# A four-layer convolution kernel: the start of its attention layer rearranged (factors spread by TensorE, input in eight pieces, small loads on another queue, first step's multiply on VectorE)

## The chip, the cores and the metric

The kernel runs on one core of one Trainium2 chip. The metric is the device time of one execution in microseconds; three runs of the kernel before gave a median of 10,728.44 us (10,727.74 to 10,730.07). The engines are named as the profile names them: PE (matrix products; PEld is its weight load), DVE (VectorE), ACT (ScalarE), POOL (GpSimd) and SP (SyncE, which issues DMA loads and stores). SPq and ACTq are the queues on which SP and ACT issue DMAs; q1 in the profile is SP's, q10 is ACT's.

## The reference

A tensor x of 8 images, 16 channels, 128 by 128 pixels, float32, goes through four layers, each of the form x + layer(groupnorm(x)), with 8 groups of two channels. The first layer, which the change concerns, makes of each pixel three tokens (one for each column of its 3x3 window, wrapped at the edges), each of 48 values (16 channels times three rows), and runs a small transformer block over them:

```python
x = _fold_to_kernels(in_x)               # (B*H*W, 3, 48)
qkv = _ln(x) @ w_attn.T                  # 4 heads of 12
att = softmax(einsum('nhtd,nhsd->nhts', q, k) / sqrt(12))
x = x + (att @ v) @ w_attn_proj.T
x = x + gelu(_ln(x) @ w_fc.T) @ w_fc_proj.T
x = sum(_ln(x), axis=1)
out = einsum('bhwc,oc->bohw', x, conv_w) + conv_b
```

The second layer is a gated 1x1 convolution (five 16x16 weights, five biases), the third a convolution of rational functions, the fourth one of splines. The change leaves the mathematics of all four as it is.

## The kernel before

**Constants and small loads.** The constants lie in one array; `const` holds those of the later layers and `const0` those of layer 0 (`center` to `last`). ACT's queue first issues `const` (L133), then small loads: the helper `rep` (L168 to L173) copies a bias of 16 values into each 16 of 128 partitions, one DMA each, for the two biases `bias0` and `bias3` and the five `b1s`; L224 puts each 16x16 weight of the second layer eight times on the diagonal of a 128x128 tile, the first two of them transposed. Together these are 96 DMAs. None of them is read in layer 0 except `bias0`, when a step's result is stored.

**Statistics.** The input arrives as eight pieces `xj` of 128 partitions by 2,048 values (1 MB each), loaded by SP (L240) into a pool of two buffers; VectorE takes four `bn_stats` of each (L242). `group_stats` (L178) aggregates them, sums over channel pairs with two small matmuls, takes the root on ACT (`lut`, L152) and gives a factor `rs0` and a shift `d0` for each of the 128 image-channel rows.

**Factors.** Layer 0 works on pairs of images: 128 partitions are two images with three rows of a window and 16 channels each, in two halves of 64, and which image lies in which half alternates with the number of the pair. The factors therefore have to move to other partitions. They are written to memory (`aff_d`, L267) and read back by 24 DMAs of SP (L275) into `aff`. For each of four pairs k, VectorE places the shifts in `shift` (L317), PE forms `pb` (L321), and VectorE makes `wcen`, the centering weights with the normalization folded in (L322). Behind the factors on the queues, weights are loaded (`wqkv`, `wfc`, `wcv`, `wpc`, `wfp`, `wfq`); `centered` (L290) subtracts a mean from the last three.

**Steps and rounds.** A step is four image rows of all images; 32 steps pass through a software pipeline in rounds n = -2 ... 34. In one round step n+2 (`ahead`) is loaded and centered, step n+1 (`then`) gets its queries, keys and values, its products with `multiply` and its scores, step n (`new`) its attention (`attend`), projection and half of its hidden layer, step n-1 (`old`) the rest, and step n-2 (`done`) is stored. So round 0 is the first with a `new` and has no `old`, and round -1 has a `then` and no `new`. `load` (L411) fills `xin`, one buffer of four pairs, by six DMAs for each pair (more at the image's edge); `center` (L425) reads it, so the rows of the next step wait for the centering of the one before. `multiply` (L464) forms the products of queries with shifted keys on POOL into tiles of a pool named "large" of five buffers, which `scores` (L479) sums on PE. `attend` (L511) spreads one row of the attention by three matmuls into banks 1 to 3, VectorE multiplies them with the values (L518), and POOL adds the three products of one pair (L527). `project` (L529) reads the sum; `two` (L336) hands out pairs of the eight PSUM banks, from bank 4 on while a `new` step attends.

**Order.** PE's instructions of layer 0 are tied in the order of the text by `in_turn`; VectorE's and POOL's long ones too, each on its own chain. All other instructions are put in order when the program is built: on each engine and queue, what is written earlier goes first among what is ready.

Of the kernel before, what the change touches and what calls it, by code (L numbers as in the profile page):

```python
# [36 lines left out]
def _constants():  # L37
# [23 lines left out]
    for k in range(4):  # L61
        for u in range(3):
            v = 32 * (2 * (k % 2) + u % 2) + 8 + 4 * (u // 2) + 2 * (k // 2)
            last[v + g, u, 32 * k + 16 * g + c] = 1.0
    parts["spread"] = spread.reshape(128, 512)
    parts["bcast"] = bcast.reshape(128, 640)
    parts["last"] = last.reshape(128, 384)
    p = np.arange(BC)
    parts["pair"] = 0.5 * (p[:, None] // 2 == p[None, :] // 2)
# [31 lines left out]
def kernel(  # L101
# [64 lines left out]
    nc.gpsimd.memset(eps_t, EPS)  # L166

    def rep(vec, n, name):  # L168

        t = cpool.tile([n * C, 1], F32, name=name)  # L170
        for b in range(n):
            nc.scalar.dma_start(t[b * C : (b + 1) * C], vec.unsqueeze(1))
        return t  # L173
# [45 lines left out]
    for n in range(5):  # L219
        t = cpool.tile([BC, BC], F32, name=f"w1_{n}")  # L220
        nc.gpsimd.memset(t, 0.0)
        for b in range(B):
            r = slice(b * C, (b + 1) * C)
            nc.scalar.dma_start(t[r, r], w1[n].rearrange("i o -> o i") if n < 2 else w1[n])  # L224
        w1s.append(t)
        b1s.append(rep(b1[n], B, f"b1_{n}"))
# [7 lines left out]
    with ExitStack() as l0:  # L234
        wp = l0.enter_context(tc.tile_pool(name="w0", bufs=1))
        with tc.tile_pool(name="x0", bufs=2) as xp:
            bn0 = xp.tile([BC, NCH, 6], F32, name="bn0", bufs=1)
            for j in range(8):
                t = xp.tile([BC, HW // 8], F32, name="xj")
                nc.sync.dma_start(t, xv[:, bass.ts(j, HW // 8)])  # L240
                for i in range(NCH // 8):
                    nc.vector.bn_stats(bn0[:, NCH // 8 * j + i], t[:, bass.ts(i, 512)])  # L242
            mean0, _, rs0, d0 = group_stats(bn0, "0")
        lo, hi = _WHERE["center"][1], _WHERE["last"][2]
        const0 = wp.tile([128, hi - lo], F32, name="const0")
        nc.scalar.dma_start(const0, const_in[:, lo:hi])

# [14 lines left out]

        aff_d = dram.tile([BC, 2], F32, name="aff_d")
        aff_s = wp.tile([BC, 2], F32, name="aff_s")
        nc.vector.tensor_copy(aff_s[:, 0:1], rs0)
        nc.vector.tensor_copy(aff_s[:, 1:2], d0)
        nc.sync.dma_start(aff_d, aff_s)  # L267
        aff = zeros([2, NP], "aff")
        for a in range(2):
            src = aff_d[:, a : a + 1].rearrange("(d p g c) a -> p g c (d a)", p=2, g=2, c=C)  # L270
            for odd in range(2):
                for g in range(2):
                    for i in range(3):
                        r = 64 * (g ^ odd) + 16 * i
                        nc.sync.dma_start(aff[r : r + 16, a, odd::2], src[odd, g])  # L275

# [4 lines left out]
        for i in range(3):  # L281
            for g in range(2):
                r = slice(64 * g + i * 16, 64 * g + i * 16 + 16)
                nc.scalar.dma_start(
                    wqkv[r, :, :E], w0_qkv[i].rearrange("c (n o) -> c n o", n=3)
                )
                nc.sync.dma_start(wfc[r], w0_fc[i])
                nc.scalar.dma_start(wcv[r, g * 16 : (g + 1) * 16], w0_conv[i])

        def centered(t):  # L290

            s = wp.tile([128, 1], F32, name="csum", bufs=3)
            nc.vector.tensor_reduce(s, t[:, :E], AX.X, ALU.add)
            nc.vector.tensor_scalar_mul(s, s, -1.0 / E)
            nc.vector.tensor_scalar(t[:, :E], t[:, :E], s, None, ALU.add)
# [3 lines left out]
        for g in range(2):  # L299
            nc.sync.dma_start(wpc[64 * g : 64 * g + E, :E], w0_proj)  # L300
            nc.scalar.dma_start(wfq[64 * g : 64 * g + 64, :E], w0_fcp[128:192])
# [23 lines left out]

        xin = wp.tile([128, NP, 512], F32, name="xin")
        nc.gpsimd.memset(xin, 1.0)
        act = l0.enter_context(tc.tile_pool(name="act0", bufs=1))
# [74 lines left out]
        class Step:  # L403
# [7 lines left out]
            def load(self, d):  # L411
                for k in (2 * d, 2 * d + 1):
                    for g in range(2):
                        for i in range(3):
                            r, lo = 64 * (g ^ (k % 2)) + i * 16, self.h0 + i - 1
                            a = max(-lo, 0)
                            z = min(H - lo, 4)
                            src, dst = x_in[2 * k + g], rows(xin[r : r + 16, k])
                            nc.sync.dma_start(dst[:, a:z], src[:, lo + a : lo + z])
                            if a:  # L420
                                nc.sync.dma_start(dst[:, 0:a], src[:, H - a : H])
                            if z < 4:
                                nc.sync.dma_start(dst[:, z:4], src[:, 0 : 4 - z])

# [38 lines left out]

            def multiply(self, d):  # L464

                for k in range(2):
                    parts = []
                    for at, n in ((0, 3), (3, 2)):
                        t = large("pd")
                        ins = nc.gpsimd.tensor_mul(  # L470
                            t[:, :n].rearrange("p n (a b) -> p n a b", a=4),
                            rows(self.q[d][:, k]).unsqueeze(1).to_broadcast([128, n, 4, W]),
                            windows(self.k[d][:, 4 * k : 4 * k + 4], at, n),
                        ).ins
                        in_turn("pool", ins)
                        parts += [t[:, i] for i in range(n)]
                    self.pd[2 * d + k] = parts
# [32 lines left out]

            def attend(self, k, j):  # L511

                for u in range(3):
                    r = slice(32 * u, 32 * u + 32)
                    pe(banks[:, 1 + u], spread[r, k], self.att[r, j], start=True, stop=True)
                y = large("y")
                v = self.v[k // 2][:, 4 * (k % 2) : 4 * (k % 2) + 4]
                ins = nc.vector.tensor_mul(  # L518
                    y.rearrange("p n (a b) -> p n a b", a=4),
                    banks[:, 1:4].rearrange("p n (a b) -> p n a b", a=4),  # L520
                    windows(v, j, 3),
# [134 lines left out]
        for n in range(-2, NCH + 3):  # L656
# [40 lines left out]
            if ahead:  # L697
                for d in range(2):
                    ahead.load(d)
            ring["from"] = 2 if new else 1  # L700
            for i, fs in enumerate(between):
                if new:
                    new.attend(i // 3, i % 3)
                for f in fs:
# [6 lines left out]
            if then:  # L711
                then.multiply(0)
                then.qkv(1)
                then.multiply(1)
            if ahead:
# [769 lines left out]
```

## Time and profile before

| | |
|---|---|
| Median of three runs | 10,728.44 us |
| The profiled execution, whole | 10,728.63 us |
| Its span in the profile | 10,726.8 us |
| Mean granted clock of TensorE | 0.976 |
| Busy over the span: PE, DVE, ACT, POOL | 84%, 81%, 80%, 52% |
| First bn_stats begins, last one ends | 6.59 us, 46.3 us |
| Root on ACT begins | 63.00 us |
| First centering on PE begins | 86.05 us |
| First multiply on POOL begins, last of that step ends | 104.42 us, 126.7 us |
| First attend on PE begins, first projection begins | 144.67 us, 174.68 us |
| Step 0's result added to the input (L588) | 369.3 us |
| Last step's result added to the input | 3,417.6 us |

The span is what the profiler saw between the first and the last instruction; the execution's own time lies 1.8 us above it. The last two rows bound the steady part of layer 0: 31 rounds. The rest of the span, some 7,300 us, belongs to the other three layers. A line of the timeline gives start, duration, engine, line of the source, operation and tiles, how many were put together, and in brackets how long the engine had been idle before it and what ended that.

### The profile page before, as it was taken

The page shows a single profiled execution, that of the slowest core. Times are in us where ns is not written, and L with a number is a line of the kernel's source. Part 1 is how long each engine was busy: PE and PEld are TensorE (multiplying, and loading weights), DVE is VectorE, ACT ScalarE, POOL GpSimd, SP SyncE. Part 2 cuts the span into 40 slices and gives each one's busy share as a digit, 9 for nine tenths or more (in the row PEclk, how much of TensorE's full clock was granted, in tenths as well). Part 3 has the DMA queues.
Part 4 walks back from the last instruction along what each step waited for, and adds up shares of the span by engine and source line. Part 5 has one row for each costly group of instructions (what it writes and reads, how often), then busy time and mean ns, then how long its engine had stood idle before and what let it go on. Part 6 is the DMA issues. An engine that isn't in the chain of part 4 may idle for free.

```text
span 10726.8 us, 191623 instructions
## 1 busy us (share of the span) xinstructions
PE 9016.0 (84%) x81588; PEld 2440.6 (23%) x81588; DVE 8720.1 (81%) x6829; ACT 8613.6 (80%) x7107; POOL 5545.4 (52%) x2681
## 2 busy tenths in 40 slices
PE   4999999999998568888888888888888888888799
PEld 1222222222222112222222222222222222222222
DVE  3555555555555569999999999999999999999977
ACT  2555555555554679999999999999999999999988
POOL 3655655555553555555555555555555555555522
PEclk8999999999999789999999999999999999999999
DMA  1000000000001320000000000000000000000022
GB/s 50 14 14 12 16 13 14 15 13 13 16 10 44 96 87 8 14 7 8 14 8 7 14 8 8 14 7 8 14 8 8 14 8 7 14 8 8 7 62 61
DMA packets 189456, 205.04 MB, mean 19 GB/s; under 512 B 46776, under 2 KB 155448, under 8 KB 186552
## 3 DMA queue, kind: packets, MB, share of 16 engines
q1 hardware_dynamic: 179944, 190.68, 6.7%
q8 instruction: 641, 10.50, 0.4%
q10 hardware_dynamic: 8656, 2.11, 0.1%
q14 instruction: 215, 1.76, 0.1%
HBM read 107.15 MB, written 60.04 MB: 16 GB/s over the span
## 4 chain that ended last, share of the span: by engine, by line
DVE 42%; PE 24%; issue 21%; ACT 7%; POOL 3%; DMA 2%; SPq 1%; ACTq 0%; DVEq 0%; POOLq 0%
PE banks L360 18%; DVE u L1030 15%; DVE pn L1030 10%; DVE u L1034 8%; DVE y L518 2%; DVE t L1020 2%; PE pn L971 2%; PE pd L971 2%; PE acc L1334 1%; POOL y L527 1%; DVE x L538 1%; ACT u L152 1%; DMA yd<-y 1%; ACT hid L152 1%; SPq L1298 1%
## 5 line engine op out<-in xcount | busy, mean ns | idle before, releaser
L1043 POOL TENSOR_TENSOR v<-t,u 128x1280 f32<-128x1280 f32 x1152 | 3374.3, 2929 | 2990.1 <-DVE t L1020 2960.8
L971 PE MATMUL pd<-f,wb 32*64 32x512 f32 x18432 | 2518.4, 610 | 332.8 <-ACT t L1009 301.0
L1020 DVE SCALAR_TENSOR_TENSOR t<-t,u 128x2048 f32<-128x2048 f32 x1152 | 2637.5, 2289 | 34.8 <-ACT u L152 25.2
L1009 ACT ACTIVATE t<-pd 128x1024 f32<-128x1024 f32 x2304 | 2348.6, 1019 | 86.6 <-POOL v L1043 42.3
L152 ACT ACTIVATE u<-u 128x2048 f32<-128x2048 f32 x1152 | 2200.4, 1910 | 0.0
L152 ACT ACTIVATE u<-t 128x2048 f32<-128x2048 f32 x1152 | 2192.1, 1903 | 0.0
L971 PE MATMUL pn<-f,wa 32*64 32x512 f32 x18432 | 1324.8, 624 | 938.4 <-DVE u L1034 938.1
L1030 DVE TENSOR_TENSOR u<-pn,u 128x1280 f32<-128x1280 f32 x1152 | 1718.1, 1491 | 39.4
L152 ACT ACTIVATE hid<-banks 128x1024 f32<-128x1024 f32 x576 | 571.4, 1023 | 1046.6 <-PE banks L360 1044.7
L527 POOL TENSOR_TENSOR y<-y 128x1536 f32<-128x1536 f32 x256 | 894.7, 3495 | 830.9 <-DVE y L518 830.9
L1062 PE MATMUL acc<-u,const 128*32 128x512 f32 (+2 forms) x13824 | 1118.9, 456 | 0.0
L1030 DVE TENSOR_TENSOR pn<-pn,u 128x768 f32<-128x768 f32 x1152 | 1104.2, 959 | 0.0
L1034 DVE SCALAR_TENSOR_TENSOR u<-t,pn 128x768 f32<-128x768 f32 x1152 | 1087.6, 944 | 0.0
L518 DVE TENSOR_TENSOR y<-banks,vp 128x1536 f32<-128x1536 f32 x384 | 672.9, 1752 | 274.0 <-PE banks L360 271.8
L971 PEld LDWEIGHTS pd<-f,wb 32*64 32x64 f32 x18432 | 512.1, 131 | 1610.2 <-ACT t L1009 1548.7
L1062 PE MATMUL acc<-v,const 128*32 128x512 f32 (+1 forms) x9216 | 749.9, 443 | 1.5 <-POOL v L1043 1.5
L544 ACT ACTIVATE sq<-x 128x1024 f32<-128x1024 f32 x384 | 397.9, 1054 | 412.3 <-DVE x L538 289.7
L971 PEld LDWEIGHTS pn<-f,wa 32*64 32x64 f32 x18432 | 279.5, 131 | 1947.3 <-DVE u L1034 1936.7
L470 POOL TENSOR_TENSOR pd<-q,kp 128x1536 f32<-128x1536 f32 (+1 forms) x256 | 693.6, 2733 | 8.0 <-PE banks L360 7.2
L360 PE MATMUL banks<-att,const 32*128 32x512 f32 x2304 | 497.3, 667 | 173.5 <-DVE att L509 95.9
L360 PE MATMUL banks<-h,wfc 64*128 64x512 f32 (+1 forms) x3072 | 618.4, 631 | 14.5 <-DVE h L606 14.5
L606 DVE TENSOR_TENSOR h<-banks,x 128x1024 f32<-128x1024 f32 x192 | 232.6, 1211 | 435.5 <-ACT hid L152 230.4
(182 smaller groups left out, 8068.9 us busy)
## 6 DMA issues: line engine op xcount, KB each, us to landing
f<-yd SPq DMA_DIRECT2D x512, 101.6 KB
yd<-y SPq DMA_DIRECT2D x320, 130.0 KB
xin<-in_x SPq DMA_DIRECT2D x752, 32.0 KB
four<-sil SPq DMA_DIRECT2D x256, 65.0 KB
xj<-in_x SPq DMA_DIRECT2D x8, 1024.0 KB
xl<-in_x SPq DMA_DIRECT2D x32, 256.0 KB
x1d<-xl SPq DMA_DIRECT2D x32, 256.0 KB
x<-x1d SPq DMA_DIRECT2D x8, 1024.0 KB
```

The source lines that it names most:

```text
L152: ins = nc.scalar.activation(out_, in_, func, **kw).ins
L360: in_turn("pe", mm(*args, skip_group_check=True, **kw).ins)
L470: ins = nc.gpsimd.tensor_mul(t[:, :n].rearrange("p n (a b) -> p n a b", a=4), rows(self.q[d][:, k]).unsqueeze(1).to_broadcast([128, n, 4, W]),
L518: ins = nc.vector.tensor_mul(y.rearrange("p n (a b) -> p n a b", a=4), banks[:, 1:4].rearrange("p n (a b) -> p n a b", a=4), windows(v, j, 3),
L527: in_turn("pool", nc.gpsimd.tensor_add(self.y[k], self.y[k], y).ins)
L971: yield mm(p[64 * (u % 2) : 64 * (u % 2) + 64, u // 2], w[lo : lo + 32, q % 2, n].rearrange("p c f -> p (c f)"), fs[g * NP + q][lo : lo + ...
L1009: in_turn("act", nc.scalar.activation(self.t[:, ab], self.pd, AF.Abs).ins)
L1020: ins = nc.vector.scalar_tensor_tensor(self.t, self.t, 1.0, self.u, op0=ALU.add, op1=ALU.mult).ins
L1030: in_turn("dve", nc.vector.tensor_mul(u if cols.start else p, p, u).ins)
L1034: ins = nc.vector.scalar_tensor_tensor(u, t, 2.0, p, op0=ALU.subtract, op1=ALU.mult).ins
L1043: ins = nc.gpsimd.tensor_mul(self.v, t, u).ins
L1062: ins = mm(accs[k][32 * q : 32 * q + 32, lo % 512 : (hi - 1) % 512 + 1], gather[:, int(part == 1), g], flat(c.u)[:, ab, lo:hi] if src is N ...
```

## The change

It has seven parts.

1. The factors no longer go through memory. Two new constants, `pairs` (which pair of images a row belongs to) and `pick` (which partitions it goes to), let VectorE make two scaled copies and PE spread them with two matmuls; one copy brings the result to `aff`.
2. The pool of input pieces has eight buffers instead of two.
3. `const0` is loaded and `xin` allocated and set to one before the pieces instead of behind the statistics and the weights.
4. The 96 small loads are collected in a list and issued by SP in round 0, behind the loads of step 2 in the text. `wfc` and `wpc` are loaded by ACT instead of SP.
5. `centered` is ordered behind the copy to `aff`.
6. Step 0's rows are loaded by SP for even pairs and by ACT for odd ones.
7. The `multiply` of the first step (round -1, with no `new`) is done by VectorE instead of POOL; the first seven `attend` calls of round 0 alternate between banks 1 to 3 and 4 to 6.

```diff
+    pick = np.zeros((128, 2, 128))
+    for odd in range(2):
+        for i in range(3):
+            pick[p, odd, 64 * (p // C % 2 ^ odd) + 16 * i + p % C] = 1.0
+    parts["pick"] = pick.reshape(128, 256)
+    parts["pairs"] = 1.0 * (p[:, None] // 32 == np.array([0, 2, 1, 3])[None, :])
...
         for b in range(n):
-            nc.scalar.dma_start(t[b * C : (b + 1) * C], vec.unsqueeze(1))
+            loads.append((t[b * C : (b + 1) * C], vec.unsqueeze(1)))
...
-            nc.scalar.dma_start(t[r, r], w1[n].rearrange("i o -> o i") if n < 2 else w1[n])
+            loads.append((t[r, r], w1[n].rearrange("i o -> o i") if n < 2 else w1[n]))
...
-        with tc.tile_pool(name="x0", bufs=2) as xp:
+        lo, hi = _WHERE["center"][1], _WHERE["last"][2]
+        const0 = wp.tile([128, hi - lo], F32, name="const0")
+        nc.scalar.dma_start(const0, const_in[:, lo:hi])
+        xin = wp.tile([128, NP, 512], F32, name="xin")
+        nc.gpsimd.memset(xin, 1.0)
+        with tc.tile_pool(name="x0", bufs=8) as xp:
...
-        aff_d = dram.tile([BC, 2], F32, name="aff_d")
-        aff_s = wp.tile([BC, 2], F32, name="aff_s")
-        nc.vector.tensor_copy(aff_s[:, 0:1], rs0)
-        nc.vector.tensor_copy(aff_s[:, 1:2], d0)
-        nc.sync.dma_start(aff_d, aff_s)
-        aff = zeros([2, NP], "aff")
-        for a in range(2):
-            src = aff_d[:, a : a + 1].rearrange("(d p g c) a -> p g c (d a)", p=2, g=2, c=C)
+        aff = wp.tile([128, 2, NP], F32, name="aff")
+        both = wp.tile([128, 2, NP], F32, name="both")
+        nc.vector.tensor_scalar_mul(both[:, 0], k0("pairs"), rs0)
+        nc.vector.tensor_scalar_mul(both[:, 1], k0("pairs"), d0)
+        with tc.tile_pool(name="ps_aff", bufs=1, space=PSUM) as pp:
+            pa = pp.tile([128, 2, 2, NP // 2], F32, name="pa")
+            pick = k0("pick").rearrange("p (o m) -> p o m", o=2)
             for odd in range(2):
-                for g in range(2):
-                    for i in range(3):
-                        r = 64 * (g ^ odd) + 16 * i
-                        nc.sync.dma_start(aff[r : r + 16, a, odd::2], src[odd, g])
+                src = both[:, :, 2 * odd : 2 * odd + 2]
+                mm(pa[:, odd], pick[:, odd], src, start=True, stop=True)
+            ready = nc.vector.tensor_copy(
+                aff.rearrange("p a (d o) -> p a d o", o=2), pa.rearrange("p o a d -> p a d o")
+            ).ins
...
-                nc.sync.dma_start(wfc[r], w0_fc[i])
+                nc.scalar.dma_start(wfc[r], w0_fc[i])
...
-            nc.vector.tensor_reduce(s, t[:, :E], AX.X, ALU.add)
+            ins = nc.vector.tensor_reduce(s, t[:, :E], AX.X, ALU.add).ins
+            tc.add_manual_dep(ins, ready.name, order, reason="not needed so soon")
...
-            nc.sync.dma_start(wpc[64 * g : 64 * g + E, :E], w0_proj)
+            nc.scalar.dma_start(wpc[64 * g : 64 * g + E, :E], w0_proj)
...
+                    eng = nc.scalar if self.h0 == 0 and k % 2 else nc.sync
...
-                            nc.sync.dma_start(dst[:, a:z], src[:, lo + a : lo + z])
+                            eng.dma_start(dst[:, a:z], src[:, lo + a : lo + z])
...
-                        ins = nc.gpsimd.tensor_mul(
+                        ins = (nc.vector if engine == "dve" else nc.gpsimd).tensor_mul(
...
-                        in_turn("pool", ins)
+                        in_turn(engine, ins)
...
-                    pe(banks[:, 1 + u], spread[r, k], self.att[r, j], start=True, stop=True)
+                    pe(banks[:, at + u], spread[r, k], self.att[r, j], start=True, stop=True)
...
+            if n == 0:
+                for dst, src in loads:
+                    nc.sync.dma_start(dst, src)
...
-                    new.attend(i // 3, i % 3)
+                    new.attend(i // 3, i % 3, 4 if not old and i < 7 and i % 2 else 1)
...
-                then.multiply(0)
+                then.multiply(0, "pool" if new else "dve")
                 then.qkv(1)
-                then.multiply(1)
+                then.multiply(1, "pool" if new else "dve")
```

## The prediction

> **What bounds the kernel now.** I read the page first: 10,726.8 us of span, and its chain of waits is spread over work of all four layers. The change touches the start of layer 0 only, whose later rounds run the same code as before, so the question is how much of the start can be cut, and whether the cut reaches the end. The table by stage comes next (columns: stretch, length, then busy time and instruction count of PE, PEld, DVE, ACT and POOL, then granted clock, DMA share, GB/s).
>
> ```profile
> 0.00:46.40 46.40, 0.00 (x0) 0.00 (x0) 20.42 (x36) 0.00 (x0) 3.48 (x18) 1.00 0.61 192
> 46.40:86.00 39.60, 3.58 (x12) 2.93 (x12) 5.67 (x30) 2.77 (x3) 0.76 (x4) 1.00 0.21 50
> 104.00:129.00 25.00, 14.80 (x84) 2.76 (x80) 2.62 (x3) 7.70 (x10) 22.63 (x16) 0.95 0.09 20
> 145.00:175.00 30.00, 16.58 (x52) 4.10 (x53) 12.42 (x8) 0.00 (x0) 13.70 (x4) 0.50 0.00 1
> 310.00:400.00 90.00, 83.37 (x448) 23.25 (x440) 49.89 (x39) 45.26 (x48) 44.92 (x25) 0.96 0.04 11
> ```
>
> In the first two rows nothing computes: loads, then 39.6 us between the last statistics and the first centering. In the third POOL alone is full; in the fourth two engines take turns. By the last row PE is 93% busy: a steady round (some 101 us) can only be moved, not shortened. The timeline shows what the first 86 us wait for.
>
> ```profile
> 57.93 3.75 ACTq L172 DMA_DIRECT2D b<-in_b  x8
> 61.71 1.28 ACT L152 ACT_TABLE_LOAD   x1 [61.71 <-DMA b<-in_b]
> 63.00 0.20 ACT L152 ACTIVATE s<-var 128x1 f32<-128x1 f32 x1
> 64.45 0.35 SPq L267 DMA_DIRECT2D aff_d<-aff_s  x1
> 68.50 13.25 SPq L275 DMA_DIRECT2D aff<-aff_d  x24
> 82.96 0.15 DVE L317 COPY shift<-aff 64x1 f32<-64x1 f32 x1 [1.24 <-DMA aff<-aff_d]
> ```
>
> The variance is ready at 49.5, but the square root stands behind 96 small loads on ACT's queue; then 24 small copies bring the factors back from memory. SP's own waits say that the queues are tied:
>
> ```profile
> SPq L287 <- DMA xj<-in_x: 7.7, 1, 7.7
> SPq L287 <- DMA w<-in_w: 7.6, 1, 7.6
> SPq L419 <- DMA b<-in_b: 2.4, 8, 0.6
> ```
>
> L287 loads a weight that depends on neither. The load at 22.58 waited for one issued at 16.56, seven or eight issues earlier counting both queues: only about eight loads are in flight over SP and ACT together. The groups by shape (86 to 210 us) price the rest:
>
> ```profile
> L527 POOL TENSOR_TENSOR y<-y 128x1536 f32<-128x1536 f32 x8 | 27.5, 3439 | 29.2 <-DVE y L518 29.2
> L470 POOL TENSOR_TENSOR pd<-q,kp 128x1536 f32<-128x1536 f32 x7 | 21.6, 3089 | 0.0
> L518 DVE TENSOR_TENSOR y<-banks,vp 128x1536 f32<-128x1536 f32 x12 | 21.1, 1757 | 22.4 <-PE banks L360 22.4
> L470 POOL TENSOR_TENSOR pd<-q,kp 128x1024 f32<-128x1024 f32 x6 | 14.2, 2366 | 0.0
> L444 DVE TENSOR_TENSOR hn<-banks,xc 128x1024 f32<-128x1024 f32 x4 | 4.9, 1220 | 6.8 <-ACT vp L357 5.5 <-PE banks L360 1.2
> ```
>
> **The input.** Each 1 MB piece costs four bn_stats in 2.47 us, 19.8 of the 46.3 us until the last ends; the rest is landing. Two pieces asked for together landed at 6.59 and 9.31, so 2.7 us a piece in a busy stream; later pairs under ACT's loads were 3.5 and 3.7 apart. With eight buffers: first landing 6.6, seven more at 2.7, and const (0.26 MB) and const0 (now issued first, some 1.0 MB) in the same stream at 3.4, so the last lands at 28.9; plus 2.5 is 31.4. At 3.7 a piece, 39.6. The in-flight limit keeps the queue full but the pieces share it with weights, so I take 32.5, near the fast end: **gain 13.8** (bounds 7 to 17).
>
> **The factors.** The store, the 24 copies and the two aff_s copies go. Before, centering begins 39.7 us after the last bn_stats (86.05 less 46.33). After: aggregate and two small matmuls to the variance 3.2 as now (49.5 less 46.33); root and five VectorE operations 1.24 (63.00 to 64.24); two scalings 0.3; two small matmuls at the 0.58 of L184's group, 1.1; copy 0.2; the nine operations of centered, now placed behind this copy, 1.1 (two tiles took 0.83 at 77.4); shift and wcen for four k, 4.0 (82.96 to 86.05 is 3.1 for three). Sum 11.1. Whether the root finds ACT's queue free is not sure: it now carries 2 constants, 23 weights and half of step 0's rows, 41 issues at 0.45 to 0.6, thus 18 to 25 us, but tied to SP's pieces by the flight limit: 145 loads on both took 62 us before, the 66 that now stand ahead (8 pieces, 2 constants, 23 weights, 32 rows, xl) take 28 by that pace, against a variance at 35.7. I add 1 (bounds 0 and 8). **Gain 27.6** (20 to 28.6). Behind the new copy on VectorE stand centered and then shift, and PE's centering waits for both, so they are counted in full. const0 has landed by 30, so the new matmuls do not wait for it; xin's memset, now earlier, is 1.8 us on an idle POOL. Step 0's rows cost nothing while they land beside the pieces; uncovered they would cost 16 issues at 0.5, 8 us.
>
> **First multiply.** On POOL it ran without a break of note from 104.42 to 126.77. On VectorE, which this stage leaves free, the nearest rows are 1757 and 1220 ns (L518, L444): 2.98 for each of four k, 11.9; between them come hn (1.22) and the two operations of the variance (1.4), which also hold back the buffers of the fourth k; I get the end at 119.0, with the matmuls after it as before. **Gain 8** (6 to 10). POOL keeps only the edge copies of k and v (0.20 each, 0.8 for a pair), and they run beside the products. In a later round a POOL addition that started at 369.48 beside a VectorE operation on SBUF operands (L588) took 3.82 instead of 3.44; by that row the copies cost some 0.4 more, which I leave in the bounds. In the Trainium skill, GPSIMD Engine Reference, Key points, POOL shares its SBUF interfaces with VectorE and contends with instructions that read two SBUF inputs. The multiply is of that kind; an estimate from this rule, each pair's copies held for one product, makes the gain 6 instead of 8.
>
> **First attend.** Seven attends take 4.0 each: 2.1 of PE, 1.76 of VectorE, in turn on one set of banks (clock 0.50). With two sets the matmuls of one run beside the product of the other, a pace of 2.1. But then POOL is late: four additions of 3.44 must be done before the first projection, behind the second product at 6.0: 6.0 + 4 x 3.45 = 19.8, where the projection now starts 30.0 after the first attend (144.67 to 174.68). **Gain 10.1** (8 to 11.5). Here the Trainium skill, TensorE: Matmul & The Clock Gate, part 1, says that some 3.4 us of sustained work doubles PE's clock; the denser run would then go at 1.13 an attend, as at 177.98. By that the pace falls to 1.76 and the sum stays, since POOL sets it.
>
> **The moved loads.** The 96 small loads go to SP, written after step 2's rows. An order on a queue isn't the text's: step 0's xl, written for round 2, was issued at 62.59, ahead of the factors' store. So the small loads will fill SP's first idle time, after its 8 pieces and 16 rows. The pieces keep most of the eight places until 29, which leaves perhaps 35 of the 66 behind; two queues at 0.47 each need 8 us for these: SP is free around 37. Step 1's rows can start when step 0's centering has read xin, about 46.6; before, they landed just in time (PE waited 0.8 and 0.6 us at 93.34 and 95.05), and PE's order puts that centering ahead of step 0's scaling, so any lateness is paid in full. Queued behind are also step 2's rows, which have 60 us in hand (issued by 112, read at 180). All 96 at 0.47 are 45 us, until 82: 36 late. None ahead: 0. From the last piece to the factors' store the old queues placed 84 loads in 28 us, 3 per us, so some 40 go in front: 19 us from 37, until 56. **Loss 8 to 9; I take 8** (0 to 36).
>
> **Sum.** 13.8 + 27.6 + 8 + 10.1 - 8 = 51.5. The profiled execution took 10,728.6 (span 10,726.8 and 1.8 around it), the median of the runs is 10,728.4, the same within 0.2. Forecast **10,677**.
>
> **Rivals.** (a) The small loads stand ahead of step 1's rows almost whole: loss 30 instead of 8, 10,699. For it: SP is idle long enough, and 96 loads from 37 last past 80. Against: the rows come earlier in the program. (b) The cut is larger: rows in time and pieces at 2.7: 13.8 + 1.1 + 28.6 + 10 + 10.1 = 63.6, 10,665. For it: 339 GB/s in one stretch (25 to 30 us, a busy share of 0.89). Against: SP's issue time. (c) The cut is made but lost later, the kernel slower: the order of copies and squares that are not tied "in turn" is set when the program is built, so a new start can settle into another rhythm. Step lengths, by the xl loads, now repeat 103.1, 99.6, 101.1, mean 101.3. If all 31 rounds took the 104.3 that one early round took (985.0 less 880.7), it would cost 93: 10,770. It decides from 1.7 us a round (51.5 over 31), measurably from 2.3. For it: the pattern only settles after 1,083 us, so it depends on the start; against: until 2,500 it then repeats within 0.2, and PE is 93% full, which leaves little to lose. (d) The change does nothing, since layer 0's rounds keep to something outside them: 10,728. For it: SP serves them all; against: from 310 to 400 PE idles 6.6 of 90 us, too little for a wait on anything else.
>
> **Chances.** Forecast (within 10 of 10,677) 0.55, (a) 0.18, (b) 0.15, (c) 0.07, (d) 0.05. No change is within 0.2%, 21 us, about what a measurement here can tell. Faster: the forecast, (b), most of (a): 0.87; same 0.08; slower 0.05, from (c). The range, 10,655 to 10,702, takes in (a) and (b); the forecast's own is 10,664 to 10,689.
>
> **What would show it.** The last bn_stats ends near 32; the root starts within 2 us of the variance; centering at about 45; VectorE carries pd of the first step, done 15 us after its first; the attends start 2.1 apart and the first projection waits on POOL; PE waits some 8 us for xin at step 1's first centering; the xl loads keep their distances, each 50 us earlier. A wait for xin beyond 20, or distances above 102.5 in the mean, would overturn the number.

## The result and the profile after

The changed kernel takes 10,681.28 us (median of 6 runs, 10,677.06 to 10,687.15) against 10,728.78 (6 runs, 10,727.74 to 10,734.18) of the kernel before: a ratio of 0.9957, 95% interval 0.9947 to 0.9967, 47.5 us less. The profiled execution took 10,685.92 us, its span 10,684.1. The median lies 4 us above the predicted 10,677, inside the forecast's own range of 10,664 to 10,689. The stages add up to the right sum, but several of its terms were wrong.

The table by stage of the changed kernel, its columns as in the table of before (the stretches are the new places of the same stages):

```profile
0.00:40.20 40.20, 0.00 (x0) 0.00 (x0) 19.82 (x33) 1.28 (x1) 3.46 (x17) 1.00 0.74 259
40.20:50.90 10.70, 4.37 (x17) 3.83 (x17) 6.16 (x34) 1.49 (x2) 0.75 (x4) 1.00 0.13 25
68.90:89.90 21.00, 14.73 (x83) 3.58 (x80) 13.92 (x11) 7.44 (x10) 4.87 (x7) 0.84 0.18 25
105.80:123.80 18.00, 15.46 (x48) 4.40 (x48) 12.18 (x7) 0.00 (x0) 12.16 (x4) 0.50 0.09 17
260.00:350.00 90.00, 83.33 (x442) 23.35 (x434) 50.25 (x40) 44.64 (x47) 44.93 (x24) 0.96 0.04 11
```

Row by row against before: the input takes 40.2 us instead of 46.4; from the last statistics to the first centering 10.7 instead of 39.6; the first multiply is VectorE's now (13.92 busy, POOL 4.87 instead of 22.63); in the first attends PE works 15.46 of 18.0 us instead of 16.58 of 30; the steady round is what it was. The stages, each from the mark in the row above to its own, in the two timelines:

| from, to | before | after | gain |
|---|---|---|---|
| start, last bn_stats ends | 46.33 | 40.13 | 6.2 |
| first centering on PE | 39.72 | 10.74 | 29.0 |
| first product of step 0 | 18.37 | 18.05 | 0.3 |
| first copy of the attention's scores | 24.30 | 20.94 | 3.4 |
| first attend | 15.95 | 15.94 | 0.0 |
| attend that follows the first projection | 33.31 | 21.62 | 11.7 |

Together 50.6 us; in the second round the lead is 51.8. It then stays, as the reciprocal of the softmax shows, which comes once a round (instructions of that line: times, shortest, median and longest in ns, first and last start); first line before, second after:

```profile
L508 DVE RECIPROCAL mx<-mx x32: 3348/3350/3350, 139.4 to 3289.0; 96x512 f32<-96x512 f32 x32
```

```profile
L520 DVE RECIPROCAL mx<-mx x32: 3348/3350/3351, 100.5 to 3237.4; 96x512 f32<-96x512 f32 x32
```

At the first round the lead is 38.9 (the attends are still to come), at the last 51.6. So the rounds kept their rhythm. In the third layer (the rational functions; a recorded expectation below calls it the second) one VectorE line comes 1,152 times. Its first instance starts 51.4 us earlier than before, its last only 45.1 earlier. Before and after:

```profile
L1020 DVE SCALAR_TENSOR_TENSOR t<-t,u x1152: 2272/2292/2296, 3584.3 to 10157.2; 128x2048 f32<-128x2048 f32 x192
```

```profile
L1036 DVE SCALAR_TENSOR_TENSOR t<-t,u x1152: 2272/2292/2346, 3532.9 to 10112.1; 128x2048 f32<-128x2048 f32 x192
```

From first to last these are 6,572.9 and 6,579.2 us, with the same code. What these 6.3 us are is taken up below.

The timeline of the root and the factors after (start, length, engine, line, tiles, in brackets the idle time before and what ended it):

```profile
43.15 0.16 DVE L204 TENSOR_SCALAR var<-pv 128x1 f32<-128x1 f32 x1 [0.68 <-PE pv L202]
43.34 0.20 ACT L159 ACTIVATE s<-var 128x1 f32<-128x1 f32 x1 [6.75 <-DVE var L204]
44.02 1.80 SPq L714 DMA_DIRECT2D bias<-in_b_conv  x4
45.98 0.17 DVE L285 COPY aff<-pa 128x8 f32<-128x8 f32 x1 [1.13 <-PE pa L284]
50.87 3.62 PE L371 MATMUL banks<-xin,wcen 64*64 64x512 f32 x16 [0.38 <-DVE wcen L335]
52.87 1.24 SPq L431 DMA_DIRECT2D xin<-in_x  x3
```

The root starts right behind the variance: ACT had been idle for 6.75 us, its queue empty. Of the 96 small loads SP issued only four ahead of step 1's rows (44.02); the rows (52.87) start as soon as the centering has read `xin`. The other 92 run from 77 to 121 us, where nobody needs the queue. SP's own waits in the first 60 us (in all, times, longest) show why the pieces came no faster:

```profile
SPq L255 <- DMA xj<-in_x: 12.2, 2, 7.6
SPq L255 <- DMA wcv<-in_w_conv: 8.9, 2, 5.3
SPq L255 <- DMA xin<-in_x: 6.3, 1, 6.3
```

L255 loads the pieces, which depend on nothing. Yet they waited for `wcv`, a small weight, and for a row of step 0, both on ACT's queue. The trace's semaphores (the counters by which an instruction waits for another) show how: all loads of SP and ACT together take eight semaphores in turn, and each load waits until the one it takes is free. So the limit of eight is one of this program; whether the hardware has one too is not shown.

The first seven attends start on PE every 2.0 us. The eighth goes back to the banks of the seventh and waits 1.94 us for VectorE; the projection follows it without a gap, has to wait in the middle (four of its matmuls start before 125, the fifth at 125.39) for the fourth of POOL's additions, which ends at 125.33, and the next attends take 1.13 each:

```profile
111.48 13.85 POOL L539 TENSOR_TENSOR y<-y 128x1536 f32<-128x1536 f32 x4 [10.98 <-DVE y L530]
117.77 2.08 PE L371 MATMUL banks<-att,const 32*128 32x512 f32 x6 [0.16 <-DVE y L530]
121.79 2.08 PE L371 MATMUL banks<-att,const 32*128 32x512 f32 x6 [1.94 <-DVE y L530]
123.81 3.69 PE L371 MATMUL banks<-y,wpc 64*64 64x512 f32 x16
127.42 1.13 PE L371 MATMUL banks<-att,const 32*128 32x512 f32 x6
```

### The profile page after: what moved, and what is told of

Its sections match the earlier page's. It is cut to its first block, busy times and chain, and to the rows that moved or that the text cites. A ratio compares the mean times of both kernels' runs of the same rounds, so it can differ in the third digit from the quotient of the medians.

```text
span 10684.1 us, 191585 instructions
## 1 busy us (share of the span) xinstructions
PE 9021.8 (84%) x81592; PEld 2443.1 (23%) x81592; DVE 8730.9 (82%) x6838; ACT 8610.2 (81%) x7107; POOL 5524.9 (52%) x2672
## 4 chain that ended last, share of the span: by engine, by line
DVE 42%; PE 25%; issue 21%; ACT 7%; POOL 3%; DMA 2%; SPq 1%; ACTq 0%; DVEq 0%; POOLq 0%
PE banks L371 18%; DVE u L1046 15%; DVE pn L1046 10%; DVE u L1050 8%; DVE y L530 2%; PE pn L987 2%; DVE t L1036 2%; PE pd L987 2%; ACT u L159 1%; POOL y L539 1%; DVE x L550 1%; PE acc L1350 1%; DMA yd<-y 1%; ACT hid L159 1%; SPq L1314 1%
## 5 line engine op out<-in xcount | busy, mean ns | idle before, releaser
L482 POOL TENSOR_TENSOR pd<-q,kp 128x1536 f32<-128x1536 f32 x248 | 671.9, 2733 | 8.3 <-PE banks L371 7.4
```

The source lines that it names most:

```text
L482: ins = (nc.vector if engine == "dve" else nc.gpsimd).tensor_mul(t[:, :n].rearrange("p n (a b) -> p n a b", a=4), rows(self.q[d][:, k]).un ...
```

## The experiments

Each run starts from the changed kernel unless it says otherwise. The total moves by 10 us from one execution to the next with no edit (10,677.06 to 10,687.15 above), and most of these runs have one execution, so the readings are marks of the start-up. These move too: over the eight profiles that leave the input as it is, the last bn_stats ends at 38.4 to 40.1, and the changed kernel's two profiles have their first attend at 105.80 and 101.79.

### Pieces first

```diff
+        def behind(dma):
+            tc.add_manual_dep(dma.ins, last_piece.name, order, reason="pieces first")
-                nc.scalar.dma_start(wfc[r], w0_fc[i])
+                behind(nc.scalar.dma_start(wfc[r], w0_fc[i]))
```

and so for every weight of layer 0 and every row of step 0.

> The layer's own weights and step 0's rows are put behind the issue of the eighth input piece on their queues; nothing else changes. Theory A, the pieces wait for ACT's small loads through the limit of about eight loads in flight over both queues: without those loads between them the eight pieces are issued with no wait for wcv or xin, their statistics come 2.7 to 3.2 us apart instead of 4.5, and the last bn_stats ends at 31 to 34 us instead of 40.1. Rival B, the stream of bytes sets the pace: the last bn_stats stays at 39 to 41 and the waits move to other names. In both, 55 DMAs then stand behind the pieces, on two queues at 0.5 each some 14 us, so the first centering may be bound by rows and weights: by A it is at 44 to 48 instead of 50.9, by B at 51 to 58.

The last bn_stats ended at 29.0, better than theory A's range; SP issued all eight pieces by 7.1 us, the first had landed at 6.1 and the last at 26.5, 2.9 apart in the mean. Theory A holds: 11.1 of 40.1 us were lost to small loads that took places in flight. It was the places and not the small loads' own traffic: seven of them were issued between 11.2 and 24.0 us here too, while the pieces landed at this pace. But the first attend came at 103.79, which the changed kernel also reaches without the edit. In the chain of waits of this run (start, length, what) stands where the gain went:

```profile
40.08 2.14 PE banks L374 x6
42.22 0.15 SPq L437
42.37 0.04 issue
42.41 1.78 DMA xin<-in_x
44.22 0.38 ACTq L439
...
49.03 2.08 PE banks L374 x4
```

L437 on SP is a row of step 1, which had to wait until PE had read `xin`; L439 on ACT is a row of step 0, which waited for that load's place in flight. A load that waits for an engine holds up another queue's loads that need no engine.

### Two buffers again

```diff
-        with tc.tile_pool(name="x0", bufs=8) as xp:
+        with tc.tile_pool(name="x0", bufs=2) as xp:
```

> The input pool has two buffers again instead of eight. Theory (after the run with the pieces first): in the changed kernel the limit in flight and not the buffers held the pieces, so the eight buffers alone gained little, and the last bn_stats ends within 2 us of 40.1. Rival: the buffers made the 6.2 us of gain: 44 to 47.5.

The last bn_stats ended at 44.85, the first attend came at 110.75: the theory fell, the rival stands. The limit in flight is not the only bound; with two buffers a piece is asked for later, and the places go to other loads. So 4.7 of the 6.2 us are the buffers' (4.7 to 6.4 against the eight profiles), and the pieces-first run shows another 11 behind them.

### Small loads back on ACT

```diff
-            loads.append((t[b * C : (b + 1) * C], vec.unsqueeze(1)))
+            nc.scalar.dma_start(t[b * C : (b + 1) * C], vec.unsqueeze(1))
```

and so for the weights.

> The 96 small loads go back to ACT, ahead of the weights and of the odd pairs' rows; the factors still go over TensorE. Theory: the root's place behind ACT's issues made some 13.5 of the 29 us that the factors gained (29.0 less the 15.5 by which the way from the root to the first centering became shorter, 23.05 to 7.53), so here the root waits again, and worse, since weights and rows of step 0 now stand behind the 96 on the same queue: the root no earlier than 57, the first centering at 64 to 85 instead of 50.9, and the pieces are held longer too (last bn_stats at 40 to 48). Rival: the small loads hide under the pieces; then the root starts within 2 us of the variance and the first centering stays within 3 us of 50.9.

The last bn_stats ended at 41.3, the root started at 64.40, the first centering at 72.89 and its second half at 84 to 90, since the odd pairs' rows stood behind the 96 loads and the weights. First attend 142.82, within 2 us of the kernel before (144.67).

```profile
62.64 0.44 ACTq L248 DMA_DIRECT2D const<-in_const  x1
63.11 1.28 ACT L159 ACT_TABLE_LOAD   x1 [63.11 <-DMA b<-in_b]
64.40 0.20 ACT L159 ACTIVATE s<-var 128x1 f32<-128x1 f32 x1
```

With the other six parts in place, this one still decides 37 us, or 41 against the changed kernel's second profile.

### Small loads ahead of step 1's rows

```diff
+            if n == -1:
+                for dst, src in loads:
+                    nc.sync.dma_start(dst, src)
             if ahead:
                 for d in range(2):
                     ahead.load(d)
-            if n == 0:
-                for dst, src in loads:
-                    nc.sync.dma_start(dst, src)
```

> The 96 small loads are written one round earlier, ahead of step 1's rows on SP. Theory, any lateness of these rows is paid in full, and it is only the place on SP's queue that made the move cost nothing: SP is busy with them from 44 to 87 or 89 (0.47 each), step 1's rows are issued some 35 us later than 52.87, PE waits 30 to 38 us for xin at step 1's first centering, and first attend is at 135 to 145 instead of 105.8. Rival 1: there is slack of 10 us or more between these rows and the multiply: 110 to 130. Rival 2: PE's work on step 0 goes on without them: within 3 us of 105.8.

First attend at 140.68, and PE's wait is the one named:

```profile
84.12 3.65 SPq L711 DMA_DIRECT2D b<-in_b  x8
87.88 7.29 SPq L431 DMA_DIRECT2D xin<-in_x  x16
90.67 3.34 PE L371 MATMUL banks<-xin,wcen 64*64 64x512 f32 x4 [34.01 <-DMA xin<-in_x]
```

Lateness of these rows is paid in full: 35.0 us later on SP, 34.9 at the first attend. The move cost nothing because of the loads' place, not for want of a price.

### Factors through memory

```diff
+        nc.sync.dma_start(aff_d, aff_s)
+                        nc.sync.dma_start(aff[r : r + 16, a, odd::2], src[odd, g])
-                mm(pa[:, odd], pick[:, odd], src, start=True, stop=True)
```

and what goes with it, as in the kernel before.

> The factors go through memory again (one store, 24 copies); queues, buffers and loads stay as in the changed kernel. Theory: the round trip itself is worth the 15.5 us between the two ways from root to first centering (23.05 before, 7.53 after), so the root stays within 2 us of the variance at 43 and the first centering comes at 64 to 68 instead of 50.9. Rival: the price of the round trip came from the 96 loads that shared the limit in flight with it; on an empty queue the 24 copies take some 8 us, and the centering is at 57 to 61. Second rival: SP's first small loads go ahead of the copies, and it is at 75 or later.

```profile
42.62 0.20 ACT L159 ACTIVATE s<-var 128x1 f32<-128x1 f32 x1 [6.36 <-DVE var L204]
44.07 0.35 SPq L279 DMA_DIRECT2D aff_d<-aff_s  x1
47.97 11.18 SPq L287 DMA_DIRECT2D aff<-aff_d  x24
```

The centering came at 63.49, just short of the theory's range: from root to centering 20.9 us instead of 7.5. So the round trip through memory makes 13.3 of the 29.0 us. (Its 24 copies took 11.18 us here and 13.25 before, where more loads ran beside them.) Of the other 15.7, 13.5 are the root's place on ACT, the wait from 49.51 to 63.00 in the kernel before that is 0.03 here; the last 2.2 are the longer way from root to centering before (23.05 instead of 20.87).

### First multiply on POOL

```diff
-                then.multiply(0, "pool" if new else "dve")
+                then.multiply(0, "pool")
```

and so for the second half.

> The first step's multiply goes back to POOL, the rest as changed. The time from the first product to the copies of the attention was 24.3 us before and 20.9 after. Theory: the move to VectorE is worth these 3.4 us, since behind the products stand the variance and 24 score matmuls in either case: here first attend 2.5 to 4.5 us later than the 105.8 of the changed kernel. Rival 1, the prediction's 8 us is there but was lost to something else that changed at the same time (start of the products, another clock): then 7 to 9 later. Rival 2, nothing: within 1 us.

First attend at 106.90, 1.1 us later; but this execution's pieces came earlier (last bn_stats 38.5 instead of 40.1), so the stage must be read: first product to first attend 39.9 us. In the changed kernel it is 36.9, and over the nine profiles that have this stage unchanged (the changed kernel's two among them) it is 35.4 to 37.1. So the move is worth 2.8 to 4.6: the theory, and not the 8 of the prediction.

### Variance first, then pinned

```diff
-                then.multiply(1, "pool" if new else "dve")
+                if new:
+                    then.multiply(1, "pool")
...
-                r = var.finish()
+                r = var.finish(pinned=then and not new)
...
+            if then and not new:
+                then.multiply(1, "dve")
```

The second run alone has the line with `pinned`, which ties L409 and L411 into VectorE's chain.

> In the first step the second half of VectorE's multiply is written behind the end of the variance, so that the two variance operations (L409, L411), which stood at 80.97 behind three products, come one product earlier and the scores' scaling is ready sooner. In the changed kernel the time from first product to first attend is 36.9 us, and PE waits 3.8 us for the variance's result before the 24 score matmuls. Theory, this chain and not the products set the end of the stage: 34.5 to 35.5. Rival, the last product sets it in any case (it ends 3.2 us after the variance): 36.5 to 37.5. Second rival, an operation of VectorE now stands behind one that waits: over 38.

> As the run with the variance first, but the two variance operations are now tied into VectorE's chain, ahead of the second half of the products. There one product still ran between them, and the variance's result came 13.3 us after the first product, as in the changed kernel (13.5), so that run decided nothing. Theory, the 24 score matmuls wait for the variance's result and run 8.2 us from there: with the operations tied it comes 11.5 to 12 us after the first product, and first product to first attend falls from 36.8 or 36.9 to 34.9 to 35.9. Rival, the products: VectorE now idles some 3 us before the variance and its last product ends later than 16.6 after the first, so the stage stays at 36.5 to 38.

The first run gave 36.8 us for the stage, the second 35.9. In the first, a product still ran between the two operations. In the second they stood together, but the variance's result came 13.2 us after the first product, no sooner than the 13.5 before: PE's matmuls ahead of it took 4.50 us instead of 2.81, at a lower clock. Both values lie within what this stage does without an edit (35.4 to 37.1), so they settle neither theory. In the combined kernel below, which has the same tie, these matmuls took 2.81 us: the result came 11.5 us after the first product and the stage took 34.2, under that range. This speaks for the theory, from one execution. What the profile does show is the order: PE waits 3.8 us for the variance's result, and only then runs the 24 score matmuls, which write a bank that the variance is read from.

```profile
81.69 0.69 DVE L411 SCALAR_TENSOR_TENSOR rstd<-banks,r 128x512 f32<-128x512 f32 x1
82.43 8.20 PE L371 MATMUL banks<-pd,const 128*32 128x512 f32 x24 [3.82 <-DVE rstd L411]
84.39 1.23 DVE L482 TENSOR_TENSOR pd<-q,kp 128x1024 f32<-128x1024 f32 x1 [2.01 <-PE banks L371]
```

That is the changed kernel. The last product waits for PE there to free a buffer, so PE, not VectorE, ends the stage.

### One set of banks

```diff
-                    new.attend(i // 3, i % 3, 4 if not old and i < 7 and i % 2 else 1)
+                    new.attend(i // 3, i % 3, 1)
```

> All attends of round 0 use banks 1 to 3 again. In the changed kernel the first seven start on PE 2.0 apart, the first projection comes 18.0 after the first attend (123.81 less 105.80), and the next round of attends 21.6 after it (127.42); before these were 4.0, 30.0 and 33.3. Theory: the second set alone is worth this, so pace 4.0, next attends 33 to 34 after the first, 11 to 12 us lost. Rival: POOL's additions, now without the products ahead of them, or another start bound this stretch; then 22 to 28.

Starts on PE 4.0 apart, the first projection 30.0 and the next attends 33.0 us after the first attend. With the second set the next attends come 21.6 to 22.9 after it over all profiles, so the set alone is worth 10.1 to 11.4. The theory holds.

### Fewer loads of weights

```diff
-                behind(nc.scalar.dma_start(wfc[r], w0_fc[i]))
+            behind(nc.scalar.dma_start(wfc[r], w0_fc.rearrange("i c o -> (i c) o")))
```

with `r` now all 48 rows of a half; so for `wqkv` and `wcv`, on top of the pieces first.

> As the run with the pieces first, and 18 loads of weights on ACT become 6 (three rows of the window at once). There step 0's odd rows stood behind 23 weights on ACT and, through the limit in flight, behind a row of step 1 on SP that itself waited for PE (5.1 us, centering interrupted from 42 to 49). Theory, issues and this tie took back 9 of the 11 us: with 12 issues fewer the odd rows are issued by 32 to 37, the centering is not interrupted by more than 1.5 us, and first attend is at 94 to 98 instead of 103.8 there and 105.8 in the changed kernel. Rival 1: the tie stays, since the rows still stand behind SP's: 101 to 105. Rival 2: the merged loads land later than they save in issues: over 105.

First attend at 99.21, between the theory's range and the first rival's. The centering was not interrupted (PE 40.57 to 44.5 in one piece), all rows were issued by 38.3. What the theory left out: the way from first centering to first product took 21.7 us instead of 18.1. A table load of ACT (1.28), which had stood in idle time, fell into the chain, and PE ran at the lower clock there (four scaling matmuls in 2.08 instead of 1.13 us).

### All three, and the changed kernel again

Pieces first, fewer loads of weights, and the variance tied ahead of the second half of the products; beside it the changed kernel with no edit.

```diff
+            behind(nc.scalar.dma_start(wfc[r], w0_fc.rearrange("i c o -> (i c) o")))
...
+                if pinned:
+                    in_turn("dve", a)
+                    in_turn("dve", b)
```

> Pieces first, six loads of weights instead of 18, and the variance tied ahead of the second half of the products. Theory, the parts add: first attend at 97.5 to 99 (99.2 with the loads alone, less the 1.0 that the tie gave), the lead over the changed kernel of 7 to 8 us stays from the second round to the end of layer 0, and the median is 10,672 to 10,676, ratio to before 0.9945 to 0.9955. Rival: the later layers, which take up to 10 us more or less from one execution to the next with the same code, hide it; the lead is there at the end of layer 0 and the median is within 4 us of the changed kernel's.

> The changed kernel once more, as the measure of what one execution differs from the next and for the comparison with the run beside it. Theory, the 6.4 us by which the second layer was longer in the changed kernel's profile (6,579.3 against 6,572.9, first to last of the same VectorE line) are such a difference and no effect of the change: first attend within 2.5 us of 105.8, the second layer anywhere from 6,570 to 6,580, median 10,677 to 10,684. Rival, the new start puts the second layer into a slower rhythm: 6,579 or more again.

The combined kernel: median 10,667.15 us (5 runs, 10,665.80 to 10,669.83), ratio to before 0.9941, interval 0.9929 to 0.9954. The changed kernel beside it on the same chip: 10,685.36 (5 runs, 10,681.85 to 10,685.81), ratio 0.9957, interval 0.9944 to 0.9971. The two sets of runs do not overlap, 18.2 us apart at the median. The combined kernel beats both. First stages of it:

```profile
0.00:29.80 29.80, 0.00 (x0) 0.00 (x0) 19.81 (x33) 0.00 (x0) 3.47 (x17) 1.00 0.86 334
29.80:40.50 10.70, 4.34 (x17) 3.79 (x17) 6.21 (x34) 1.49 (x2) 0.76 (x4) 1.00 0.27 66
```

The same statistics in 29.8 us, at 334 GB/s instead of 259. First attend at 94.93; the lead over the changed kernel's first profile is 10.9 in the first round and 10.6 in the last (over the second 6.9 and 11.9). At the first of the third layer's lines (3,525.1) 7.8 of it are left, and over the second profile 5.9. The theory had the sign right and the size too small: the third layer, where nothing was edited, adds 7 us, so that, as far as these profiles tell, 10 to 12 of the 18.2 us arise behind that line and stay unexplained.

The third layer, from first to last of the line shown above, took 6,579.2 and 6,578.9 us in the two profiles of the changed kernel, 6,571.9 in the combined one, and 6,570.1 with the multiply on POOL, a kernel whose instruction order on PE and ACT is the changed kernel's throughout and on VectorE and POOL differs in the first step alone. Over all kernels with this code it is 6,570.1 to 6,579.9. The difference builds up over thousands of microseconds, in steps of at most 1.2, and not at one place. Whether it belongs to a kernel (the two like values speak for it) or to an execution stays open: the last run's theory allows 6,578.9, and its rival is a tenth away.

## Why the prediction was right, and where it was not

**The input, 13.8 predicted, 6.2 measured** (7.2 in the second profile), below the lower bound of 7. The step that failed is "The in-flight limit keeps the queue full but the pieces share it with weights, so I take 32.5, near the fast end". The tie between the queues had been read correctly, and then used on the wrong side: the limit counts loads, not bytes, so 23 weights and 16 rows on ACT took places from 1 MB pieces. What the pieces waited for shows it in the chain of the changed kernel (start, length, what):

```profile
4.86 9.13 DMA wcv<-in_w_conv
15.25 4.56 DMA wcv<-in_w_conv
26.09 6.26 DMA xin<-in_x
```

Pieces first removed 11.1 us. The pace of 2.7 us a piece was itself near: 2.9 there, and 2.6 from the second piece on, where VectorE's own 2.47 a piece leaves little to wait for.

**The factors, 27.6 against 29.0.** Right, by its steps: variance done 3.2 us after the last bn_stats (3.2 predicted), root at once (1 allowed), centering 10.7 after the last bn_stats (11.1 plus 1). The parts are 13.3 for the round trip, 13.5 for ACT's queue and 2.2 for the slower round trip before; the second exists only with the small loads gone from ACT, as their return showed.

**First multiply, 8 against 3.4.** What failed is "I get the end at 119.0, with the matmuls after it as before". The products did shrink, from 22.3 to 16.7 us, 2.1 short of the plan as the last one waits for a buffer. The matmuls behind them did not stay: 1.9 us remained behind POOL's last product, 4.2 behind VectorE's. POOL's products came slowly enough for PE to sum them as they arrived; VectorE's are nearly all done before PE may start, since the variance's two operations now stand behind products on the same engine (result 13.5 us after the first product, 10.2 with the multiply on POOL). The Trainium skill (GPSIMD Engine Reference, Key points), by which the term would have been 6 for sharing, is right in its direction: the copies of `vp`'s edges took 1.07 and 1.19 us in the mean beside VectorE's products, 0.19 to 0.20 with the multiply on POOL, and 0.20 in the pinned run's second pair, where VectorE idled. But they stand off the path, and the missing 4.6 us are not theirs.

**First attend, 10.1 against 11.7** (10.8 in the second profile). The pace of 2.0 was as said. POOL as the next bound was half right: its fourth addition ended 19.5 us after the first attend, where the sum had 19.8, but the projection began at 18.0, because it begins with the parts that POOL has finished. What set its start is a step that the sum left out: the eighth attend, which stands ahead of it in PE's order and waits for the seventh's banks. POOL held only the matmuls after the projection's first four. The other rule weighed there, the Trainium skill's (TensorE: Matmul & The Clock Gate, Part 1), did not show in these 18 us: PE worked 15.46 of them, and the granted clock stayed at 0.50 through the stretch. The clock rose at 125.78, 4.0 us into PE's first stretch without a gap (from 121.79); the stretches before lasted 3.79 us at most. The measurement decides for the row.

**The moved loads, 8 lost, nothing measured.** The failed step is "So the small loads will fill SP's first idle time, after its 8 pieces and 16 rows", with some 40 of them in front. Four stood in front. SP issued them from 44.02 to 45.8 and then stood idle until 52.87, with the other 92 still to issue. A late input is not the reason: in the run with the pieces first, and in the two kernels built on it, SP had issued its rows by 34.7 to 35.1, earlier than the 37 assumed, idled for over 5 us, and still only three or four small loads stood ahead of step 1's rows. How many go ahead is fixed with the order when the program is built, not by SP's idle time on the chip; why that order puts four there stays open (it was eleven with two buffers and nine with the factors through memory). So rival (a) needed another order and not an earlier SP, and the run with the loads ahead of the rows shows that it would have been paid in full. Of the two waits that the prediction reads at 93.34 and 95.05, only the second, 0.6 us, is PE's for `xin`.

**The sum.** Errors: input -7.6, factors +1.4, moved loads +8.3 (a gain of 0.3 instead of a loss of 8), multiply -4.6, attend +1.6, a further 1.3 behind the first projection: +0.4 (0.3 without rounding). So 51.5 was predicted and 51.8 stood in the second round. That they agree is luck: two large errors of opposite sign, and four smaller ones. Rival (c), another rhythm, fell: the last round's lead is the second's. The predicted sum assumed that nothing would change behind layer 0. In the profiled execution 9 of the 51.6 us of lead in the last round were lost there, 6.3 of them in the third layer; where the 4 us between forecast and median lie, no profile tells.

## What to carry to other kernels

Count loads in flight, not bytes: where queues share a limit, put the large transfers that set the end ahead of small ones on every queue, merge the small ones, and look for loads that wait on an engine while others wait for their place. An engine that is twice as fast at a stage is worth what the next engine in the chain can take; look at what it did while the slow one worked. A total that comes out right proves little: check each term against its own mark.

## What the runs showed of the hardware

PE's clock makes the same code differ from run to run. The 24 score matmuls took 8.20 us in the changed kernel's first profile and 6.66 in its second (stretch, length, busy time of PE, PEld, DVE, ACT, POOL, then granted clock, DMA share, GB/s):

```profile
82.40:91.00 8.60, 8.20 (x24) 1.73 (x24) 1.23 (x1) 1.13 (x2) 0.00 (x0) 0.66 0.15 1
```

```profile
79.90:88.00 8.10, 6.66 (x24) 1.58 (x24) 1.23 (x1) 2.13 (x4) 0.00 (x0) 0.83 0.16 1
```

It is the granted clock, 0.66 and 0.83, that differs. PE waited 3.82 us ahead of both, so the history alone of the last microseconds does not tell them apart. The two traces' records of the clock tell more: it changes in steps of 3.41 us, and stood at 0.50 from 81.40 to 88.23 (two steps) in the first and from 79.23 to 82.65 (one step) in the second. The matmuls began 1.0 and 0.7 us into the low clock; why one step was enough in the second is not shown. And in the first attends 86% of busy time did not raise the clock above 0.50.
